# A fixed order for the first stage: query products, then key products, between the transposes of the input tiles

## The chip, the cores and the metric

The kernel runs on one core of a Trainium2 (trn2) chip. The metric is the device time of one execution in microseconds (us); the time of a kernel is the median of several runs. TensorE (PE) does the matrix products, VectorE (DVE) and ScalarE (ACT) the elementwise work and the copies out of PSUM, GpSimd (POOL) sums between SBUF tiles, and SyncE's queue (SP) issues all DMAs. "PEld" in the profile is TensorE's weight load.

## The reference, cut to what matters

One pre-norm transformer block on x of 1 x 1024 x 512, in float32: attention with 32 heads of 128, then a feed-forward net whose weights are signs.

```
x = x + attn(layernorm(x), wq, wkv, wo)
x = x + ffn(layernorm(x), k0, s0, k1, s1, k2, s2)

attn: q, k, v = h @ wq, h @ wkv ...          # 32 heads, 128 used columns each
      p = softmax(q k^T * 192**-0.5, causal)
      out = (p v) @ wo
ffn:  h = relu(s0 * (x @ sign(k0))) * 2 ; h = relu(s1 * (ei(h) @ sign(k1))) * 2 ; s2 * (ei(h) @ sign(k2))
```

The change touches the first layer norm, the queries and keys of the first two heads, and three small constants of the feed-forward net.

## The kernel before, in words

The 1024 tokens are 8 tiles of 128. The heads are taken in pairs. The queries, keys and values of a pair are made in seven partial products of half size each (Strassen's scheme, `products`, L313); a generator spreads these products over the softmax steps of the pair before. The first pair has no pair before it, so its queries and keys are made plainly by `qk_plain` (L284), ahead of everything else; its values come from `products(2, 0)` during the first pair's softmax steps.

**The first stage.** SP issues the loads in program order (L106 to L109): x tile 0, wq of head 0, x tile 1, wq of head 1, x tile 2, wk of head 0, x tile 3, wk of head 1, x tiles 4 to 7; then the value weights `wv` (L148), `wo` (L150), a second copy of x into `acc` (L158) and the three scalars `s_sb` (L164). A DMA may have to wait for the one eight places before it. For each tile of x, `statistics` (L201) makes mean and variance on DVE (bn_stats, bn_aggr), the root on ACT (L215) and its reciprocal on DVE (L217); `normalise` (L220) applies them on DVE; `transposed` (L226) makes four PE transposes into one PSUM bank of the pool `ps_mm`; and ACT copies that bank into `xnT` (L236). `qk_plain(0)` and `qk_plain(1)` then make, for each half of the tokens, four banks: queries of heads 0 and 1, keys of heads 0 and 1. A unit, as it is called below, is one tile of tokens in one bank: four products of 128 x 128, which the trace shows as eight matmul rows (a float32 product runs as two). Three banks are from pool `ps_st` (3 buffers), the fourth from `ps_sc`, the pool of one buffer that the softmax scores use. ACT copies each full bank to `qT` or `kT` (L306).

Then POOL makes `token_sums` (L248), four sums over `xnT` that the partial products read; the last of them overwrites a half of `xnT` in place, so it waits for the plain products. The first softmax step (`softmax_step`, L611) follows: scores on PE, minimum on DVE (L485), exponential on ACT (L496), scale (L501), and block transposes on DVE into `tb` (L507). SP exchanges blocks of `tb` into `pT` by 16 or 32 DMAs (L551), which the value product `ps_av` reads.

**What sets the order.** Each engine runs its own queue in order. A scheduler in the tile framework orders instructions that are not pinned; `pinned[0]` turns on program order for matmuls (`matmul`, L64 to L68). Before the change it is turned on after the first softmax step (L629), so the whole first stage is ordered by the scheduler. On PE it put the transposes of the tiles first, with a few products between them. PSUM has `ps_sc` 1, `ps_st` 3 and `ps_mm` 3 buffers.

Of the kernel before, what the change touches and what calls it, by code (L numbers as in the profile page):

```python
# [29 lines left out]
def kernel(  # L30
# [30 lines left out]

    pinned = [False]

    def matmul(*args, **kw):  # L64

        ins = nc.tensor.matmul(*args, **kw)  # L66
        if pinned[0]:
            tc.keep_in_program_order(ins)  # L68

    def pool(name, bufs, **kw):  # L70
        return ctx.enter_context(tc.tile_pool(name=name, bufs=bufs, **kw))
# [15 lines left out]
    def load_x(t):  # L87
        if t % TPB == 0:
            x_in.append(pairs.tile([P, TPB, D], F32, tag="pT", name=f"x_in{t // TPB}", bufs=3))
        nc.sync.dma_start(x_in[-1][:, t % TPB, :], x_v[:, t, :])  # L90

    def load_qk_weights(which, g, heads_of=range(G)):
        if (which, g) not in w_raw:
            w_raw[which, g] = pairs.tile(
                [P, G, NC, DN], F32, tag="wraw", name=f"w{'qk'[which]}{g}"
            )
        for i in heads_of:
            h = g * G + i
# [7 lines left out]
    for t in range(NT):  # L106
# [27 lines left out]
        nc.gpsimd.memset(t, 0.0)  # L134
        tb.append(t)


    def load_v_weights(g):
        wv_sb[g] = pairs.tile([P, NC, G * DV], F32, tag="wv", name=f"wv{g}", bufs=1)
        first = H * DN + g * G * DV  # L140
        nc.sync.dma_start(wv_sb[g], wkv_v[:, :, first : first + G * DV])
# [6 lines left out]
    load_v_weights(0)  # L148
    load_qk_weights(0, 1)
    load_o_weights(0)  # L150


    acc = const.tile([P, 7, TPB, DH], F32, tag="acc", name="acc")
    xs = []
    for t in range(NT):
        k, i = divmod(t, TPB)
        xs.append(acc[:, 2 * k : 2 * k + 2, i, :])
        nc.sync.dma_start(xs[t], x_v[:, t, :].rearrange("p (h d) -> p h d", h=2))  # L158

    nc.gpsimd.tensor_tensor(acc[:, 2], acc[:, 2], acc[:, 3], ALU.subtract)  # L160

    s_sb = const.tile([P, 3], F32, tag="s", name="s_sb")
    for i, s in enumerate((s0, s1, s2)):
        nc.sync.dma_start(s_sb[:, i : i + 1], s[None, :].to_broadcast((P, 1)))  # L164
    s_twice = const.tile([P, 2], F32, tag="s_twice", name="s_twice")
    nc.vector.tensor_scalar_mul(s_twice, s_sb[:, 0:2], 2.0)


    mixed = n_exc // P
    f = const.tile([P, 1], F32, tag="f", name="f")  # L170
    nc.gpsimd.memset(f, 1.0)
    nc.gpsimd.affine_select(
        out=f,
        in_=f,
        compare_op=ALU.is_gt,
        fill=inh,
        base=n_exc - mixed * P,
        pattern=[[0, 1]],
        channel_multiplier=-1,
    )  # L180
    f_twice = const.tile([P, 1], F32, tag="f_twice", name="f_twice")
    nc.vector.tensor_scalar_mul(f_twice, f, 2.0)
    f_minus = const.tile([P, 1], F32, tag="f_minus", name="f_minus")
    nc.vector.tensor_scalar_mul(f_minus, f, -1.0)

    def sign_weights(i, k, slots):

# [13 lines left out]
    def statistics(tiles, name):  # L201

        n = len(tiles)
        mv = small.tile([P, n, 2], F32, tag=f"mv{n}", name=f"mv_{name}")
        for t, xt in enumerate(tiles):
            if len(xt.shape) == 2:
                stats = small.tile([P, 6], F32, tag="stats", name=f"stats_{name}{t}")
                nc.vector.bn_stats(stats, xt)
# [4 lines left out]
            nc.vector.bn_aggr(mv[:, t, :], stats)  # L213
        std = small.tile([P, n, 1], F32, tag=f"std{n}", name=f"std_{name}")
        nc.scalar.activation(std, mv[:, :, 1:2], AF.Sqrt, bias=eps)  # L215
        rstd = small.tile([P, n, 1], F32, tag=f"rstd{n}", name=f"rstd_{name}")
        nc.vector.reciprocal(rstd, std)  # L217
        return [(mv[:, t, 0:1], rstd[:, t, :]) for t in range(n)]

    def normalise(xt, mean_rstd, name):  # L220
        xn = work.tile([P, D], F32, tag="p", name=f"xn_{name}")
        dst = xn if len(xt.shape) == 2 else xn.rearrange("p (h d) -> p h d", h=2)
        nc.vector.tensor_scalar(dst, xt, *mean_rstd, ALU.subtract, ALU.mult)
        return xn

    def transposed(t, xn, name):  # L226
        pt = ps_mm.tile([P, NC, P], F32, tag="mm", name=f"ptx_{name}{t}")
        for c in range(NC):
            nc.tensor.transpose(pt[:, c, :], xn[:, c * P : (c + 1) * P], ident)
        return pt  # L230

    xnT = const.tile([P, NC, S], F32, tag="xnT", name="xnT")
    for t in range(NT):
        xt = x_in[t // TPB][:, t % TPB, :]
        xn = normalise(xt, statistics([xt], f"a{t}")[0], f"a{t}")
        nc.scalar.copy(xnT[:, :, t * P : (t + 1) * P], transposed(t, xn, "a"))  # L236

# [39 lines left out]
    def new_qk(which, h):  # L277
        dst = (qT, kT)[which]
        dst[h] = heads.tile(
            [P, S], F32, tag=("qT", "kT")[which], name=f"{'qk'[which]}T{h}", bufs=(4, 3)[which]  # L280
        )
        return dst[h]

    def qk_plain(k):  # L284


        outs = [(which, h) for which in range(2) for h in range(G)]
        if k == 0:
            for which, h in outs:
                new_qk(which, h)  # L290
        banks = [ps_st.tile([P, QB], F32, tag="st", name=f"ps_qk{k}_{n}") for n in range(3)]
        banks.append(ps_sc.tile([P, S], F32, tag="sc", name=f"ps_qk{k}_3")[:, :QB])
        for t in range(TPB):
            tok = slice(t * P, (t + 1) * P)
            for (which, h), ps in zip(outs, banks):
                for c in range(NC):
                    matmul(
                        ps[:, tok],
                        lhsT=w_raw[which, 0][:, h, c, :],
                        rhs=xnT[:, c, k * QB + t * P : k * QB + (t + 1) * P],  # L300
                        start=(c == 0),
                        stop=(c == NC - 1),
                        skip_group_check=True,
                    )
        for (which, h), ps in zip(outs, banks):
            nc.scalar.activation(  # L306
                (qT, kT)[which][h][:, k * QB : (k + 1) * QB],
                ps,
                AF.Copy,
                scale=(-scale, 1.0)[which],  # L310
            )

    def products(which, g):  # L313

# [275 lines left out]
        if qb == 1 and g + 2 < NG:  # L590
            attn_sums(g, early=(j == 0))

    for half in range(NQB):
        qk_plain(half)
    token_sums()
    weight_sums(2, 0)

    def products_of_pair(g):
        yield from products(2, g)
        if g + 1 < NG:  # L600
# [24 lines left out]
    PRODUCT, O_PART = 2.0, 1.0  # L625
    ATTEND_AFTER = (TPB, TPB + 2)

    softmax_step(*steps[0])
    pinned[0] = True  # L629
    for i, (h, qt) in enumerate(steps):  # L630
        g, j = divmod(h, G)
        s = i % (G * NT)
# [228 lines left out]
```

## Time and profile before

| what | value |
|---|---|
| median of 3 runs | 1369.76 us (1369.54 to 1373.94) |
| profiled execution, its own time | 1375.12 us |
| span of the profiled execution | 1373.3 us |
| PE busy | 1349.3 us, 98% of the span |
| DVE, ACT, POOL busy | 803.3, 495.9, 267.9 us |
| the chain that ended last, by engine | PE 94%, SP's queue 3%, DVE 1%, DMA 1% |
| PE's first instruction | at 8.09 us |
| first row of the second product stage (X_v) | at 48.67 us |

Between the span and the execution's own time lie 1.8 us. The first stage fills the first 48 us of 1373, so the profile page's 40 slices show it as little more than one slice. It has to be read from the timeline, which lists the instructions of all engines in order of start: start, duration, engine, line, operation, names (out<-in), shape, count, and in square brackets how long the engine had been idle and what ended that. Merged rows of matmuls count their pipelined ends, so the pace of a run of matmuls is (duration less one matmul's duration) over (count less one). A second view gives the busy time of each engine and TensorE's granted clock in chosen stretches.

### The profile page before, as it was taken

The page shows a single profiled execution, that of the slowest core. Times are in us where ns is not written, and L with a number is a line of the kernel's source. Part 1 is how long each engine was busy: PE and PEld are TensorE (multiplying, and loading weights), DVE is VectorE, ACT ScalarE, POOL GpSimd, SP SyncE. Part 2 cuts the span into 40 slices and gives each one's busy share as a digit, 9 for nine tenths or more (in the row PEclk, how much of TensorE's full clock was granted, in tenths as well). Part 3 has the DMA queues.
Part 4 walks back from the last instruction along what each step waited for, and adds up shares of the span by engine and source line. Part 5 has one row for each costly group of instructions (what it writes and reads, how often), then busy time and mean ns, then how long its engine had stood idle before and what let it go on. Part 6 is the DMA issues. An engine that isn't in the chain of part 4 may idle for free.

```text
span 1373.3 us, 16933 instructions
## 1 busy us (share of the span) xinstructions
PE 1349.3 (98%) x5564; PEld 872.3 (64%) x5564; DVE 803.3 (58%) x1658; ACT 495.9 (36%) x921; POOL 267.9 (20%) x326
## 2 busy tenths in 40 slices
PE   7998999999999999999999999999999999998998
PEld 6846566575756657575665757575665757655467
DVE  3364565656556565655656565665656656675475
ACT  2343333333434333333333333333333333344322
POOL 6201221221222212022221202222120212110200
PEclk9999999999999999999999999999999999999999
DMA  5234444443444444343444434344443434334201
GB/s 184 57 89 108 102 105 109 99 119 96 111 104 113 101 108 107 97 119 96 114 103 112 108 96 116 96 110 106 111 108 95 119 93 113 98 93 110 73 1 62
DMA packets 267446, 139.33 MB, mean 101 GB/s; under 512 B 26208, under 2 KB 261216, under 8 KB 267360
## 3 DMA queue, kind: packets, MB, share of 16 engines
q1 hardware_dynamic: 267360, 138.25, 39.7%
q8 instruction: 45, 0.74, 0.3%
q14 instruction: 41, 0.34, 0.1%
HBM read 38.54 MB, written 2.10 MB: 30 GB/s over the span
## 4 chain that ended last, share of the span: by engine, by line
PE 94%; SPq 3%; DVE 1%; DMA 1%; ACT 0%; issue 0%; ACTq 0%
PE ps_av L66 18%; PE sc L66 17%; PE ps_o L66 14%; PE Y_v L66 6%; PE Y_q L66 5%; PE Y_k L66 5%; PE X_v L66 4%; PE Z_v L66 4%; PE X_q L66 4%; PE Z_q L66 4%; PE X_k L66 3%; PE Z_k L66 3%; SPq L551 3%; PE ps_qk L66 2%; PE ps_h L66 2%; PE ps_out L66 1%
## 5 line engine op out<-in xcount | busy, mean ns | idle before, releaser
L496 ACT ACTIVATE p<-p,nmax 128x128 f32<-128x128 f32 (+7 forms) x256 | 198.3, 775 | 679.1 <-DVE nmax L485 677.2
L66 PE MATMUL sc<-kT,qT 128*128 128x512 f32 (+3 forms) x768 | 290.8, 488 | 3.4 <-DVE nmax L485 2.7
L66 PE MATMUL ps_av<-pT,v 128*128 128x512 f32 x744 | 254.4, 492 | 4.6 <-DMA pT<-tb 4.6
L485 DVE CUSTOM_DVE_ANT_0 p<-sc,mask 128x128 f32<-128x128 f32 (+7 forms) x256 | 191.5, 748 | 103.4 <-PE sc L66 103.2
L507 DVE STREAM_TRANSPOSE tb<-p 128x128 f32<-128x128 f32 (+1 forms) x248 | 187.1, 769 | 83.9 <-ACT p L501 77.3
L501 ACT ACTIVATE p<-p,rtotal 128x128 f32<-128x128 f32 (+7 forms) x256 | 196.4, 772 | 92.8 <-DVE rtotal L500 92.8
L66 PEld LDWEIGHTS ps_av<-pT,v 128*128 128x128 f32 x744 | 142.7, 192 | 134.5 <-issue 105.8
L66 PEld LDWEIGHTS sc<-kT,qT 128*128 128x128 f32 x768 | 138.8, 191 | 91.9 <-issue 77.0
L448 DVE TENSOR_TENSOR acc<-acc,ps_o 128x512 f32<-128x512 f32 x190 | 128.9, 683 | 56.1 <-PE ps_o L66 50.9
L66 PE MATMUL ps_o<-wo,attn 128*128 128x256 f32 (+1 forms) x400 | 111.1, 414 | 0.0
L500 DVE RECIPROCAL rtotal<-total 128x1 f32<-128x1 f32 x256 | 40.5, 158 | 109.6 <-ACT p L496 109.3
L66 PEld LDWEIGHTS ps_o<-wo,attn 128*128 128x128 f32 x400 | 73.3, 190 | 30.6 <-issue 23.4
L409 POOL TENSOR_TENSOR at<-attn,attn 128x512 f32<-128x512 f32 x14 | 17.7, 1266 | 348.4 <-DVE attn L589 348.4
L264 POOL TENSOR_TENSOR wsumk<-wk 128x256 f32<-128x256 f32 x15 | 10.9, 727 | 306.8 <-DMA wk<-in_L_attn_wkv_dram 271.6
L589 DVE COPY attn<-ps_av 128x512 f32<-128x512 f32 x62 | 42.3, 682 | 41.2 <-PE ps_av L66 41.2
L66 PEld LDWEIGHTS X_v<-wv,xnT 128*128 128x128 f32 x512 | 62.4, 192 | 5.2
L66 PE MATMUL X_v<-wv,xnT 128*128 128x128 f32 x512 | 62.4, 275 | 0.0
L66 PEld LDWEIGHTS ps_o<-osum,at 128*128 128x128 f32 x224 | 42.5, 190 | 22.8 <-issue 19.1
L66 PE MATMUL X_q<-xnT,wq 128*128 128x512 f32 x120 | 56.4, 593 | 0.0
L66 PE MATMUL X_k<-xnT,wk 128*128 128x512 f32 x120 | 56.4, 592 | 0.0
L66 PE MATMUL ps_o<-osum,at 128*128 128x256 f32 x224 | 55.0, 379 | 0.0
L496 ACT ACTIVATION_READ_ACCUMULATOR p<-p,nmax 128x1 f32 x256 | 47.8, 187 | 0.0
(143 smaller groups left out, 1639.4 us busy)
## 6 DMA issues: line engine op xcount, KB each, us to landing
pT<-tb SPq DMA_DIRECT2D x1488, 64.0 KB, 2.0
wq<-in_L_attn_wq_dram SPq DMA_DIRECT2D x32, 256.0 KB, 3.3
wk<-in_L_attn_wkv_dram SPq DMA_DIRECT2D x32, 256.0 KB, 3.9
wv<-in_L_attn_wkv_dram SPq DMA_DIRECT2D x16, 512.0 KB, 4.0
wo<-in_L_attn_wo_dram SPq DMA_DIRECT2D x16, 512.0 KB, 3.9
x_in<-_attn_hidden_states_dram SPq DMA_DIRECT2D x8, 256.0 KB, 5.8
acc<-_attn_hidden_states_dram SPq DMA_DIRECT2D x8, 256.0 KB, 7.2
out_dram<-osb SPq DMA_DIRECT2D x8, 256.0 KB, 2.0
```

The lines of the kernel that those rows point to most:

```text
L66: ins = nc.tensor.matmul(*args, **kw)
L264: nc.gpsimd.tensor_tensor(t[:, 0], a(1, 0), a(1, 1), ALU.add)
L409: nc.gpsimd.tensor_tensor(t0, b(0, 1), b(0, 0), ALU.subtract)
L448: nc.vector.tensor_tensor(dst, dst, ps, ALU.add)
L485: nc.vector.tensor_tensor_reduce(out=p[:, :n], in0=sc[:, :n], in1=mask[:, S - n :], scale=1.0, scalar=BIG, op0=ALU.add, op1=ALU.min, accum ...
L496: nc.scalar.activation(p[:, :n], p[:, :n], AF.Exp, bias=nmax, scale=-1.0, accum_out=total)
L500: nc.vector.reciprocal(rtotal, total)
L501: nc.scalar.activation(p[:, :n], p[:, :n], AF.Copy, scale=rtotal)
L507: nc.vector.transpose(tb[qb][:, : qt + 1, :, i, :], p[:, :n].rearrange("p (c b k) -> p c b k", b=NB, k=B32))
L551: nc.sync.dma_start(pT[b * B32 : (b + 1) * B32, :, a, :, :], tb[qb][a * B32 : (a + 1) * B32, chunks, b, :, :],)
L589: nc.vector.tensor_copy(dst.rearrange("p (t a i) -> p a t i", a=NB, i=B32), ps)
```

## The change

The work is the same, but for one extra square root on a constant. Its order and its place differ:

- Loads: x tile 0, wq, x tile 1, wq, wk, wk, x tiles 2 to 4, wv, x tiles 5 to 7. `wo`, `acc` and the second pair's wq follow after the first stage in the program.
- An ACT square root on a constant `one` stands first, so that the table for it is loaded at the start.
- `qk_plain` is one function over all 32 units. It calls `normalised_input` for tile 0, 1, ... before the units 0, 2, 7, 10, 13, 16, 19, 22, and the first softmax step before unit 26. Queries of tiles 0 and 1 come before their keys; from tile 2 on, a tile's four units stand together.
- Everything in that stage is pinned to program order on every engine (`keep_order`), also statistics, roots, normalisation, transposes and the copies to `qT` and `kT`.
- The fourth bank comes from `ps_mm` and not from `ps_sc`.
- The constants of the feed-forward net (`s_sb`, `f` and what is made from them) are made at the first step of head 2.

In the order that the engines get, PE has: transposes of tile 0, units 0 and 1, transposes of tile 1, units 2 to 6, transposes of tile 2, and so on; the transposes of tile 4 stand behind unit 12 and those of tile 5 behind unit 15. ACT has: copy of tile 3, copy of bank 0 to `qT`, root of tile 4, copy of tile 4, copies of banks 1, 2 and 3, root of tile 5, copy of tile 5. DVE takes the tiles one after the other, each from statistics to normalisation. From the second softmax step on, the order of every engine is that of before, but for `f_twice`, `f_minus` and `s_twice` on DVE, `f` on POOL and the three `s_sb` loads on SP.

```diff
+    load_x(0)
+    load_qk_weights(0, 0, [0])
+    load_x(1)
+    load_qk_weights(0, 0, [1])
+    load_qk_weights(1, 0)
+    for t in range(2, NT):
         load_x(t)
-        if t < TPB:
-            load_qk_weights(t // G, 0, [t % G])
+        if t == TPB:
+            load_v_weights(0)
+    one = const.tile([P, 1], F32, tag="one", name="one")
+    nc.vector.memset(one, 1.0)
+    nc.scalar.activation(one, one, AF.Sqrt)
...
+    def ffn_constants():
+        for i, s in enumerate((s0, s1, s2)):
+            keep_order(nc.sync.dma_start(s_sb[:, i : i + 1], s[None, :].to_broadcast((P, 1))))
+        keep_order(nc.vector.tensor_scalar_mul(s_twice, s_sb[:, 0:2], 2.0))
+        keep_order(nc.gpsimd.memset(f, 1.0))
...
+    def normalised_input(t):
         xt = x_in[t // TPB][:, t % TPB, :]
         xn = normalise(xt, statistics([xt], f"a{t}")[0], f"a{t}")
-        nc.scalar.copy(xnT[:, :, t * P : (t + 1) * P], transposed(t, xn, "a"))
+        keep_order(nc.scalar.copy(xnT[:, :, t * P : (t + 1) * P], transposed(t, xn, "a")))
...
-    def qk_plain(k):
+    def qk_plain(tiles_at, last_at, last):
+        units = [(t, n) for ns in ((0, 1), (2, 3)) for t in (0, 1) for n in ns]
+        units += [(t, n) for t in range(2, NT) for n in range(2 * G)]
+        for t, n in units:
+            for new in tiles_at.get(n_units, ()):
+                normalised_input(new)
+            if n_units == last_at:
+                last()
+            n_units += 1
+            k, i = divmod(t, TPB)
+            which, h = outs[n]
+            if i == 0:
+                pl, tag = ((ps_st, "st"), (ps_mm, "mm"))[n == 3]
+                banks[n] = pl.tile([P, QB], F32, tag=tag, name=f"ps_qk{k}_{n}")
+            for c in range(NC):
+                matmul(
...
+            if i == TPB - 1:
+                keep_order(
+                    nc.scalar.activation(
...
-    softmax_step(*steps[0])
     pinned[0] = True
+    qk_plain(
+        {0: (0,), 2: (1,), 7: (2,), 10: (3,), 13: (4,), 16: (5,), 19: (6,), 22: (7,)},
+        26,
+        lambda: softmax_step(*steps[0]),
+    )
+    load_o_weights(0)
...
+        if h == 2 and qt == 0:
+            ffn_constants()
```

More of the change, by code (lines that the diff above doesn't have):

```diff
@@ L62, with keep_order, matmul @@
     pinned = [False]
-    def matmul(*args, **kw):
-        ins = nc.tensor.matmul(*args, **kw)
+    def keep_order(ins):
         if pinned[0]:
             tc.keep_in_program_order(ins)
+    def matmul(*args, **kw):
+        keep_order(nc.tensor.matmul(*args, **kw))
     def pool(name, bufs, **kw):
@@ L103, in load_qk_weights, with load_v_weights @@
             nc.sync.dma_start(w_raw[which, g][:, i, :, :], src)
-    for t in range(NT):
-        load_x(t)
-        if t < TPB:
-            load_qk_weights(t // G, 0, [t % G])
+    def load_v_weights(g):
+        wv_sb[g] = pairs.tile([P, NC, G * DV], F32, tag="wv", name=f"wv{g}", bufs=1)
+        first = H * DN + g * G * DV
+        nc.sync.dma_start(wv_sb[g], wkv_v[:, :, first : first + G * DV])
+    load_x(0)
[4 more added lines that the diff above has]
+    for t in range(2, NT):
+        load_x(t)
+        if t == TPB:
[3 more added lines that the diff above has]
+    nc.scalar.activation(one, one, AF.Sqrt)
     ident = const.tile([P, P], F32, tag="ident", name="ident")
@@ L135 @@
         tb.append(t)
[L138 to L141, printed above, removed]
     def load_o_weights(g):
@@ L146, in load_o_weights @@
         nc.sync.dma_start(wo_sb[g], wo_v[:, g * G : (g + 1) * G, :])
[L148 to L160, printed above, removed]
     s_sb = const.tile([P, 3], F32, tag="s", name="s_sb")
-    for i, s in enumerate((s0, s1, s2)):
-        nc.sync.dma_start(s_sb[:, i : i + 1], s[None, :].to_broadcast((P, 1)))
     s_twice = const.tile([P, 2], F32, tag="s_twice", name="s_twice")
-    nc.vector.tensor_scalar_mul(s_twice, s_sb[:, 0:2], 2.0)
     mixed = n_exc // P
[L170 to L179, printed above, removed]
-    )
[L181 to L184, printed above, removed]
+    f, f_twice, f_minus = (
+        const.tile([P, 1], F32, tag=n, name=n) for n in ("f", "f_twice", "f_minus")
+    )
+    def ffn_constants():
[3 more added lines that the diff above has]
+        keep_order(nc.gpsimd.memset(f, 1.0))
+        nc.gpsimd.affine_select(
+            out=f,
+            in_=f,
+            compare_op=ALU.is_gt,
+            fill=inh,
+            base=n_exc - mixed * P,
+            pattern=[[0, 1]],
+            channel_multiplier=-1,
+        )
+        nc.vector.tensor_scalar_mul(f_twice, f, 2.0)
+        nc.vector.tensor_scalar_mul(f_minus, f, -1.0)
     def sign_weights(i, k, slots):
@@ L207, in statistics @@
                 stats = small.tile([P, 6], F32, tag="stats", name=f"stats_{name}{t}")
-                nc.vector.bn_stats(stats, xt)
+                keep_order(nc.vector.bn_stats(stats, xt))
             else:
@@ L212, in statistics @@
                     nc.vector.bn_stats(stats[:, half, :], xt[:, half, :])
-            nc.vector.bn_aggr(mv[:, t, :], stats)
+            keep_order(nc.vector.bn_aggr(mv[:, t, :], stats))
         std = small.tile([P, n, 1], F32, tag=f"std{n}", name=f"std_{name}")
-        nc.scalar.activation(std, mv[:, :, 1:2], AF.Sqrt, bias=eps)
+        keep_order(nc.scalar.activation(std, mv[:, :, 1:2], AF.Sqrt, bias=eps))
         rstd = small.tile([P, n, 1], F32, tag=f"rstd{n}", name=f"rstd_{name}")
-        nc.vector.reciprocal(rstd, std)
+        keep_order(nc.vector.reciprocal(rstd, std))
         return [(mv[:, t, 0:1], rstd[:, t, :]) for t in range(n)]
@@ L222, in normalise @@
         dst = xn if len(xt.shape) == 2 else xn.rearrange("p (h d) -> p h d", h=2)
-        nc.vector.tensor_scalar(dst, xt, *mean_rstd, ALU.subtract, ALU.mult)
+        keep_order(nc.vector.tensor_scalar(dst, xt, *mean_rstd, ALU.subtract, ALU.mult))
         return xn
@@ L228, in transposed @@
         for c in range(NC):
-            nc.tensor.transpose(pt[:, c, :], xn[:, c * P : (c + 1) * P], ident)
+            keep_order(nc.tensor.transpose(pt[:, c, :], xn[:, c * P : (c + 1) * P], ident))
         return pt
     xnT = const.tile([P, NC, S], F32, tag="xnT", name="xnT")
-    for t in range(NT):
+    def normalised_input(t):
         xt = x_in[t // TPB][:, t % TPB, :]
         xn = normalise(xt, statistics([xt], f"a{t}")[0], f"a{t}")
-        nc.scalar.copy(xnT[:, :, t * P : (t + 1) * P], transposed(t, xn, "a"))
+        keep_order(nc.scalar.copy(xnT[:, :, t * P : (t + 1) * P], transposed(t, xn, "a")))
     def B(j, k):
@@ L282, in new_qk @@
         return dst[h]
-    def qk_plain(k):
+    def qk_plain(tiles_at, last_at, last):
         outs = [(which, h) for which in range(2) for h in range(G)]
[L288 to L303, printed above, removed]
-                    )
[L305 to L311, printed above, removed]
@@ new lines, in qk_plain @@
+        for which, h in outs:
+            new_qk(which, h)
+        banks, n_units = {}, 0
+        units = [(t, n) for ns in ((0, 1), (2, 3)) for t in (0, 1) for n in ns]
[13 more added lines that the diff above has]
+                matmul(
+                    banks[n][:, i * P : (i + 1) * P],
+                    lhsT=w_raw[which, 0][:, h, c, :],
+                    rhs=xnT[:, c, t * P : (t + 1) * P],
+                    start=(c == 0),
+                    stop=(c == NC - 1),
+                    skip_group_check=True,
+                )
+            if i == TPB - 1:
+                keep_order(
+                    nc.scalar.activation(
+                        (qT, kT)[which][h][:, k * QB : (k + 1) * QB],
+                        banks[n],
+                        AF.Copy,
+                        scale=(-scale, 1.0)[which],
+                    )
+                )
@@ L591, in attend @@
             attn_sums(g, early=(j == 0))
[L593 to L596, printed above, removed]
     def products_of_pair(g):
@@ L626 @@
     ATTEND_AFTER = (TPB, TPB + 2)
-    softmax_step(*steps[0])
     pinned[0] = True
+    qk_plain(
+        {0: (0,), 2: (1,), 7: (2,), 10: (3,), 13: (4,), 16: (5,), 19: (6,), 22: (7,)},
+        26,
+        lambda: softmax_step(*steps[0]),
+    )
+    load_o_weights(0)
+    acc = const.tile([P, 7, TPB, DH], F32, tag="acc", name="acc")
+    xs = []
+    for t in range(NT):
+        k, i = divmod(t, TPB)
+        xs.append(acc[:, 2 * k : 2 * k + 2, i, :])
+        nc.sync.dma_start(xs[t], x_v[:, t, :].rearrange("p (h d) -> p h d", h=2))
+    nc.gpsimd.tensor_tensor(acc[:, 2], acc[:, 2], acc[:, 3], ALU.subtract)
+    token_sums()
+    weight_sums(2, 0)
+    load_qk_weights(0, 1)
     for i, (h, qt) in enumerate(steps):
```

## The prediction

> **What bounds the kernel now.** The page says PE 98% busy, and the chain that ended last is 94% PE. So the time falls by what PE's idle or slow stretches lose, and by nothing else. I then read the timeline of the first 75 us, where the change lies. Columns: start us, duration us, engine, line, operation, names, shape, count, and in brackets the idle time before and what ended it.
>
> ```profile
> 3.52 0.69 DVE L208 BATCH_NORM_STATS2 stats_a<-x_in 128x6 f32<-128x512 f32 x1 [3.52 <-DMA x_in<-_attn_hidden_states_dram]
> ...
> 4.51 1.28 ACT L215 ACT_TABLE_LOAD   x1 [4.51 <-DVE mv_a L213]
> ...
> 6.40 0.69 DVE L208 BATCH_NORM_STATS2 stats_a<-x_in 128x6 f32<-128x512 f32 x1 [1.97 <-DMA x_in<-_attn_hidden_states_dram]
> ...
> 7.23 0.13 DVE L217 RECIPROCAL rstd_a<-std_a 128x1 f32<-128x1 f32 x1
> ...
> 7.39 0.55 DVE L223 TENSOR_SCALAR xn_a<-x_in,mv_a,rstd_a 128x512 f32<-128x512 f32 x1
> ...
> 8.09 2.13 PE L229 MATMUL ptx_a<-ident,xn_a 128*128 128x128 f32 x8 [8.09 <-DVE rstd_a L217]
> ...
> 14.27 1.09 PE L229 MATMUL ptx_a<-ident,xn_a 128*128 128x128 f32 x4 [0.25 <-ACT xnT L236]
> ...
> 15.15 2.34 PE L66 MATMUL ps_qk<-xnT,wq 128*128 128x128 f32 x10
> ...
> 19.60 1.95 PE L66 MATMUL ps_qk<-xnT,wk 128*128 128x128 f32 x16
> ```
>
> PE's first transposes wait until 8.09. Tile 0 landed at 3.52, but two things delay its normalisation: the table load of 1.28 before ACT's root, and, behind that, DVE's queue: the statistics of tile 1 stand ahead of the reciprocal of tile 0, and tile 1 lands at 6.40. The reciprocal runs at 7.23, the normalisation at 7.39.
>
> The pace matters too. Ten product rows in 2.34 us are (2.34 - 0.42)/9 = 0.213 us each; from 19.60, sixteen in 1.95 are (1.95 - 0.275)/15 = 0.112 (0.42 and 0.275 are the lengths of one such row in the two stretches). Until about 18.4 PE runs at half pace, whatever the clock column says of that time.
>
> The end of the stage:
>
> ```profile
> 44.61 1.95 PE L66 MATMUL ps_qk<-xnT,wk 128*128 128x128 f32 x16
> ...
> 46.60 0.60 ACT L306 ACTIVATE kT<-ps_qk 128x512 f32<-128x512 f32 x1 [0.29 <-PE ps_qk L66]
> ...
> 47.25 0.49 PE L66 MATMUL sc<-kT,qT 128*128 128x128 f32 x2 [0.69 <-ACT kT L306]
> ...
> 48.13 0.70 PE L66 MATMUL sc<-kT,qT 128*128 128x256 f32 x2 [0.39 <-DVE nmax L485]
> ...
> 48.67 1.95 PE L66 MATMUL X_v<-wv,xnT 128*128 128x128 f32 x16
> ```
>
> The last product row starts at 46.29, its copy to kT ends at 47.20, then come the first scores, and the second scores wait for DVE to read the first, since they share one bank: 48.13. X_v starts at 48.67.
>
> Last, I read the granted clock in stretches (length, PE busy, count, clock, DMA share, GB/s), to learn which idle stretches cost pace:
>
> ```profile
> core 0: us, PE busy (x), PEclk, DMA share, GB/s
> ...
> 107.16:110.58 3.42, 1.26 (x4) 1.00 0.45 108
> 110.58:113.99 3.41, 1.94 (x3) 0.50 0.63 176
> 113.99:117.40 3.41, 3.41 (x10) 0.50 0.38 92
> 117.40:120.80 3.40, 3.40 (x32) 1.00 0.42 100
> 1250.62:1254.03 3.41, 1.39 (x4) 1.00 0.41 98
> 1254.03:1257.44 3.41, 3.06 (x4) 0.50 0.40 97
> ...
> 1312.06:1315.47 3.41, 1.94 (x15) 1.00 0.00 0
> ```
>
> A stretch of 3.4 us with PE busy 1.26 or 1.39 (37% and 41%) is followed by half clock; one with 1.94 (57%) isn't. Full clock comes back after a stretch that is nearly full.
>
> **The start, part by part.** All product and transpose rows stay: 256 product rows and 32 transpose rows, at full pace 256 x 0.1117 + 32 x 0.1095 = 32.1 us, plus two score rows, 0.22. What changes is start, idle time and half-paced rows.
>
> First transpose: mean and variance reach ACT at 4.51. With the table loaded earlier the root ends at 4.80 (0.29); reciprocal at 4.82, normalisation 0.16 later, PE 0.70 after that (7.39 to 8.09): 5.68, so 2.41 earlier. The extra memset and root on `one` run while DVE and ACT wait for x, before 3.5. If ACT's first load were late instead, it would cost at most its 1.28.
>
> Transposes of tile 0: four at 0.213, to 6.53; the last result 0.21 later, copy 0.59, hand-over 0.08: 7.41. Two query units, 16 x 0.213, to 10.82. The wq tiles are second and fourth DMA as before and do not stop this (the second was issued at 2.19 and landed within 5.0). Tile 1: landed 6.40, root from 7.39, normalised by 8.56, so ready; transposes 10.82 to 11.67. Now PE waits for their copy: 0.88, to 12.55.
>
> The clock: PE is without a gap from 7.41 to 11.67, 4.26 us. In before the gapless stretch from 14.27 to about 18.4, 4.15 us, brought full pace. I take full pace from 12.55. Here the Trainium skill has a rule (TensorE: Matmul & The Clock Gate, Part 1: The HAM clock gate): about 3.4 us of sustained work releases the clock, but counted in free-running windows[...]. By the row, pace is full at 12.55. By the rule, a stretch of 4.26 may miss a whole window, and the next chance ends up to 3.41 later, at 15.96: that is 16 rows at half pace, 1.7 us lost. Other phases lie between. The same chance hangs over before, whose full pace came early in its possible span (17.7 to 21.1).
>
> From 12.55 on: 240 product rows 26.81, 24 transpose rows 2.63, two score rows 0.22, so 42.2 without idle time.
>
> **Where a new wait comes in.** ACT's queue is in order. The copy of bank 0 to qT stands ahead of the root of tile 4, and it needs the whole of unit 12. The transposes of tile 4 stand on PE right behind unit 12. So PE waits for: last row's result 0.275, hand-over 0.04, copy on ACT 0.51 until the next can start, root 0.29, reciprocal 0.02 + 0.16, normalisation to PE 0.70: 1.98, less one row's 0.11, so 1.87 us. The same happens at tile 5: the copies of banks 1 to 3 stand ahead of its root, the last of them needs unit 15, and the transposes follow unit 15 at once. Queued behind these on PE are all remaining units. Tiles 2, 3, 6 and 7 do not have it: no bank copy stands between, and three or more units (0.9 us each) cover their copies. Tile 2 has one unit of 0.89 to cover the copy's about 0.8. Two waits, 3.74 us.
>
> Sum: 42.2 + 3.74 = 45.95 us at the end of the last unit. The second scores can start there, since DVE read the first long before, and the table for the exponential (1.28) loads under the units. In before they start at 48.13: 2.2 us gained. In parts: 2.4 from the earlier start, 1.5 at the end (48.13 less 46.40 and 0.22 of score rows), 1.4 from half-paced rows (24 for 38, 0.10 each), less 3.3 of idle time (5.5 for 2.2): 2.0, and the rest is rounding.
>
> **What I cost at nothing.** x tiles 2 to 7 now follow the wk tiles, and wv goes ahead of tile 5. At 362 GB/s (8 to 20 us) a tile takes 0.72, so tile 2 lands near 9.3, tile 4 near 10.7, wv near 12.2 and tile 7 near 14.4. PE asks for tile 2 after about 16.5 and for tile 7 after 36. Cover: 7 us or more; without it a tile's lateness counts fully. POOL's sums: tile 7 is copied near 37.4, T[0] and T[1] take 2.35 each plus gaps, 42.3; Y_v needs them near 48.2, so 6 us of cover. The last sum, in place, starts when the units end, as before, and has the same five microseconds to its use. `wo` and `acc` land by about 22 and are used much later; wq of the second pair waits for the last query unit, as before. The fourth bank from `ps_mm` leaves two buffers for transposes that are copied within 1 us.
>
> The constants at head 2: three DMAs of about 0.4 us on SP behind the second exchange of head 1 (about 135 in before), so wk, 16 exchanges and wv behind them come 1.2 to 1.3 later. The value product that reads those exchanges starts at 154.80, the exchanges were issued by 146.6: cover 5 us or more. SP then idles before the next group. On DVE `f_twice` stands ahead of the copy of `attn` at 116.69 and waits for POOL's `f` behind sums that end at 117.41: DVE is held to about 117.8, 1.1 us. The scores at 120.92 need the minimum that would now end near 119.1: cover 1.8. If PE comes there at full clock, up to 3 us earlier, about 0.8 would show. I take 0.
>
> **Rivals.** (1) The two waits drop the clock. Each leaves a 3.4 us stretch with PE busy 1.70 of 3.41, 50%, between 41% (dropped) and 57% (kept). The skill speaks against a drop (same page, HAM oscillation: it warns only of gaps over about 3.4 us, which makes this rival nothing), but the stretch to 1254.03 was followed by half clock with one gap of 2.37, so the row decides, and it leaves a chance. Price: after the drop at 110.58 PE worked 5.35 us at half clock, 2.7 lost. Twice is 5.4 less a little where only one stretch holds enough of a wait: 5.1. Time 2.9 above before, 1372.7. It decides from below about 50% busy.
>
> (2) More is gained. Either the waits at tiles 4 and 5 turn out hidden (then -5.9, 1363.9), or the later clock drops, at 110.58 and 1254.03, fall differently as PE's stalls move against the windows: at 110 between 3.4 and 6.8 us of half pace, so up to 1 gained, at 1254 up to 1.7, together -4.9, 1364.9. Against the first stands the order of the queues, which is certain. For the second speaks that runs of before differ by 4.4 us.
>
> (3) The change does not do what it says: the first stage is DMA-bound until tile 1 lands and only PE-bound after, and the gain of the start is eaten by late full pace (-0.4): 1369.3. It shades into the likeliest case.
>
> **The numbers.** In the profiled execution the sum gives 1375.12 - 2.2 = 1372.9. That execution is 5.4 above the median; the first stage is the same program, so the difference is taken from the median: 1369.76 - 2.2 = 1367.6. Chances: the likeliest case with (3), -0.4 to -3.5, 0.60; rival (1) 0.15; rival (2) 0.20; something slow that I do not see 0.05. The measurement tells about 0.3%, 4.1 us, from no change: below 1365.65 is faster, above 1373.9 slower. Faster comes from most of (2), 0.18; slower from the worst of (1) and the unseen, 0.10; the rest is within. Range from 1364.0, near the far end of (2), to 1372.6, near the sum of (1).
>
> **What would show it.** Right: PE's first row near 5.7; X_v near 46.4 in place of 48.67; two PE idle stretches of about 1.7 to 1.9 before the transposes of tiles 4 and 5, ended by DVE's normalisation, with the bank copy ahead of the root on ACT; full pace from about 12 to 16; no idle time between the last unit and the second scores. Wrong: half clock after those waits; a wait for an x tile or for T; PE held at 120 by DVE.

## The result and the profile after

| | before | after |
|---|---|---|
| median, measured side by side | 1371.84 us (1368.84 to 1374.51) | 1374.32 us (1372.04 to 1375.44) |
| after / before | | 1.0018, 95% interval 1.0010 to 1.0025 |
| profiled execution, its span | 1375.12, 1373.3 us | 1372.76, 1370.9 us |
| first transposes | 8.09 us | 8.06 us |
| first row of X_v | 48.67 us | 48.95 us |
| X_v of pair 1 to X_v of pair 2 | 68.63 us | 67.18 us |
| X_v of pair 2 to X_v of pair 3 | 79.68 us | 79.95 us |

The change is slower by about 2.5 us, where 2.2 us of gain were forecast. The two profiled executions alone would say the opposite (1372.76 against 1375.12): one execution carries more or fewer stretches of half clock than another, and the profiled one of before had three of them. So below, times come from many runs, and traces are compared stretch by stretch.

The start, from the timeline of the changed kernel (start us, duration us, engine, line, operation, names):

```profile
2.38 5.25 POOL L150 MEMSET tb<- 128x2048 f32 x2
...
4.76 0.16 DVE L215 RECIPROCAL rstd_a<-std_a 128x1 f32<-128x1 f32 x1 [0.43 <-ACT std_a L213]
4.96 2.95 DVE L221 TENSOR_SCALAR xn_a<-x_in,mv_a,rstd_a 128x512 f32<-128x512 f32 x1
...
8.06 1.09 PE L227 MATMUL ptx_a<-ident,xn_a 128*128 128x128 f32 x4 [8.06 <-DVE xn_a L221]
```

The early table load did its part: the reciprocal comes at 4.76 where 4.82 was forecast, against 7.23 before. But the normalisation behind it takes 2.95 us instead of 0.55. It ends at 7.91, just after POOL has finished clearing the two buffers `tb` (2.38 + 5.25 = 7.63). So the transposes start where they started before.

The middle, PE's rows alone:

```profile
27.54 0.63 PE L227 MATMUL ptx_a<-ident,xn_a 128*128 128x128 f32 x4 [1.81 <-DVE xn_a L221]
...
32.66 0.63 PE L227 MATMUL ptx_a<-ident,xn_a 128*128 128x128 f32 x4 [1.81 <-DVE xn_a L221]
```

These are the two waits that were forecast at tiles 4 and 5, at 1.81 us of idle time. And the end of the stage, with the second pair's beginning:

```profile
48.52 0.60 PE L70 MATMUL sc<-kT,qT 128*128 128x256 f32 x2
...
48.95 0.72 PE L70 MATMUL X_v<-wv,xnT 128*128 128x128 f32 x5
...
117.50 0.15 DVE L181 TENSOR_SCALAR f_twice<-f 128x1 f32<-128x1 f32 x1 [3.82 <-POOL f L172]
```

The second scores follow the last unit without a pause, as forecast, but at 48.52 instead of 45.95. At head 2 DVE is held for 3.82 us until POOL delivers `f`.

The granted clock of PE in stretches (length, PE busy, count, clock, DMA share, GB/s), cut where the clock changes:

```profile
core 0: us, PE busy (x), PEclk, DMA share, GB/s
...
109.03:112.45 3.42, 1.13 (x4) 1.00 0.55 140
112.45:115.87 3.42, 3.42 (x8) 0.50 0.44 118
```

After a stretch with PE busy 1.13 of 3.42 there is one at half clock, and near 1250 there is none; before had two near 110 and one near 1250. That, and not the first stage, makes this one execution the shorter one.

### The profile page after: what moved, and what is told of

It is laid out like the page before. It is cut to its first block, busy times and chain, and to the rows that moved or that the text cites. A ratio compares the mean times of both kernels' runs of the same rounds, so it can differ in the third digit from the quotient of the medians.

```text
span 1370.9 us, 16940 instructions
## 1 busy us (share of the span) xinstructions
PE 1344.8 (98%) x5564; PEld 869.5 (63%) x5564; DVE 805.7 (59%) x1659; ACT 496.1 (36%) x922; POOL 268.8 (20%) x326
## 4 chain that ended last, share of the span: by engine, by line
PE 96%; DVE 1%; SPq 1%; DMA 1%; ACT 1%; issue 0%; POOL 0%; DVEq 0%; POOLq 0%; ACTq 0%
PE ps_av L70 18%; PE sc L70 18%; PE ps_o L70 14%; PE Y_v L70 6%; PE Y_k L70 6%; PE Y_q L70 6%; PE X_v L70 4%; PE Z_v L70 4%; PE X_q L70 4%; PE Z_q L70 4%; PE X_k L70 4%; PE Z_k L70 4%; PE ps_qk L70 2%; PE ps_h L70 2%; PE ps_out L70 1%; SPq L562 1%
## 5 line engine op out<-in xcount | busy, mean ns | idle before, releaser
L263 POOL TENSOR_TENSOR wsumk<-wk 128x256 f32<-128x256 f32 x15 | 11.4, 757 | 305.6 <-DMA wk<-in_L_attn_wkv_dram 293.8
```

The lines of the kernel that those rows point to most:

```text
L263: nc.gpsimd.tensor_tensor(t[:, 0], a(1, 0), a(1, 1), ALU.add)
```

## The experiments

Theory P: the clearing of `tb` on POOL shuts DVE's normalisation out while it runs, so the start gains nothing. Theory K: the constants at head 2, costed at nothing, hold DVE and then PE. The two waits were forecast, so they only had to be sized. Rivals: the first transposes are held by something else (rival A: landing DMAs); the constants are harmless (rival N), and the moment at which the clock changes makes the difference. The other letters are explained in the expectation ahead of each run. All ratios are to the kernel before, with 95% intervals.

**e1, the clearing later.** It is tied behind the normalisation of tile 1.

```diff
-        nc.gpsimd.memset(t, 0.0)
...
+        if t == 1:
+            for z in tb:
+                nc.gpsimd.tensor_copy(z[:, 0, 0, 0, 0:1], xn[:, 0:1])
+                nc.gpsimd.memset(z, 0.0)
```

> The changed kernel, but POOL clears the two tb tiles only after the normalisation of tile 1 (a small POOL copy that reads it comes first). Theory P: DVE's normalisation of tile 0 took 2.95 us in place of 0.55 because POOL was clearing tb from 2.38 to 7.63 and the two cannot use the memory side by side; so it takes 0.55 here, the first transposes start at 5.6 to 5.7 and X_v 2.4 us earlier than 48.95 (46.5, up to 1.7 more or less where full pace comes at another moment), and the time falls by 2.4 from 1374.3 to about 1371.9, ratio to the kernel before 1.000. Rival A: it was slow because x and weight tiles were landing just then, whatever POOL did; then it stays near 2.9 us, first transposes at 8.06, time 1374.3, ratio 1.0018.

Measured: 1373.28 us, 1.0017 (1.0008 to 1.0027). The normalisation of tile 0 took 0.55 and the first transposes started at 5.83, but X_v only at 48.19. Its timeline shows why:

```profile
15.09 5.26 POOL L237 MEMSET tb<- 128x2048 f32 x2
...
18.88 1.75 DVE L220 TENSOR_SCALAR xn_a<-x_in,mv_a,rstd_a 128x512 f32<-128x512 f32 x1
...
24.02 2.34 POOL L653 TENSOR_TENSOR acc<-acc 128x1024 f32<-128x1024 f32 x1
25.23 1.41 DVE L220 TENSOR_SCALAR xn_a<-x_in,mv_a,rstd_a 128x512 f32<-128x512 f32 x1
```

The clearing now meets the normalisation of tile 3, and the subtraction `acc`, pushed back on POOL, meets that of tile 4; each ends just after POOL's instruction does (20.63 after 20.35, 26.64 after 26.36). PE's wait ahead of tile 4 grew from 1.81 to 2.70. P holds for the start. Its worth in time is not shown by this run, since the lock was moved and not removed: 1371.9 had been expected.

**e4, the clearing done twice.** The line is repeated in a loop of two.

> The changed kernel with each tb tile cleared twice on POOL, 5.25 us more of it. Theory P: the normalisation of tile 0 ends near 13.2, the first transposes start at 13.3, everything behind is 5.2 us later: about 1379.5, ratio 1.0056 (or 1 to 2 us less where full pace comes in a better moment). Rival A: normalisation of tile 0 still ends at 7.9, ratio 1.0018.

Measured: 1380.58 us, 1.0061 (1.0041 to 1.0080).

```profile
2.37 10.45 POOL L151 MEMSET tb<- 128x2048 f32 x4
...
5.17 7.93 DVE L222 TENSOR_SCALAR xn_a<-x_in,mv_a,rstd_a 128x512 f32<-128x512 f32 x1
```

The normalisation again ends (13.10) just after the clearing (12.82), PE's first transposes move to 13.25, and the whole program follows by about 6 us (four executions). Landing DMAs as the cause are out: the loads are the same, and in e7 below, where the DMA engines were as busy from 2 to 8 us (share 1.00, in after 1.02), the normalisation took 0.55.

**e7, the clearing on DVE.** It is cut into three pieces of 1.76 us that stand in DVE's idle time.

```diff
-        nc.gpsimd.memset(t, 0.0)
...
+        for z in {2: (tb[0],), 3: (tb[1][:, :4],), 4: (tb[1][:, 4:],)}.get(t, ()):
+            keep_order(nc.vector.memset(z, 0.0))
```

> The clearing of both buffers tb leaves POOL for good: DVE does it in its own idle time, in three pieces behind the normalisations of tiles 2, 3 and 4. Theory P (in the change the clearing on POOL holds back the first normalisation): the normalisation of tile 0 takes 0.55 us at about 5.1 us, the first transposes start at 5.8 instead of 8.06, no later normalisation is held back by a clearing (only the addition acc on POOL may lengthen one, to at most 1.4 us), the two waits of 1.81 us before the transposes of tiles 4 and 5 stay, X_v starts at 46.7 instead of 48.95, and the time falls by the whole 2.2 us: 1372.1, about 1.0000 to 1.0005 of before. Rival G (the start's gain is given back inside the stage whatever is done with the clearing, because the moment of the full clock and not the first transposes sets the stage): X_v at 48 or later, 1373.3 as with the clearing moved behind tile 1, 1.0015 of before.

Measured: 1372.22 us, 1.0001 (0.9989 to 1.0014).

```profile
5.19 0.55 DVE L220 TENSOR_SCALAR xn_a<-x_in,mv_a,rstd_a 128x512 f32<-128x512 f32 x1
```

PE starts at 5.88, 0.14 after the normalisation ends (in after 0.15), and X_v at 47.19, 1.8 us sooner than after. This is P's number (1372.1), not the rival's (1373.3, or 1.0015, just above the interval): with the lock gone and not merely moved, the start's gain reaches the end.

**e2, the roots early.** Statistics, root and normalisation of tiles 4 and 5 are issued before units 12 and 13, so that they stand ahead of the bank copies in ACT's queue.

```diff
+            if n_units in (12, 13):
+                prepare(n_units - 8)
             for new in tiles_at.get(n_units, ()):
```

> The changed kernel, but statistics, root and normalisation of tiles 4 and 5 are put before units 12 and 13, ahead of the copies of the full banks on ACT. If the two PE waits of 1.81 us are in full on the path: both vanish, X_v at 45.3, time 3.6 us lower, 1370.7, ratio 0.9992. Rival: they are partly given back by the clock (the waits make no difference to the clock, but what stands behind them may meet another stretch): a change between 1.5 and 5 us.

Measured: 1370.38 us, 0.9995 (0.9987 to 1.0002). Both waits are gone. X_v stands at 47.42, not at the expected 45.3, because full clock came only at 19.43 in this trace (13.47 in after). The ratio is 0.0019 to 0.0023 below that of the changed kernel (its two comparisons gave 1.0014 and 1.0018), 2.6 to 3.2 us. The two waits had been costed at 3.74.

**e3, the constants early.** `ffn_constants()` is called before `token_sums()`, unpinned.

> The changed kernel, but the constants of the feed-forward net are made in the first stage again, in scheduler order, with their three loads behind those of acc. Theory C: at head 2 f_twice held DVE for 3.8 us (113.7 to 117.5), and that costs PE 0.2 us in the profiled execution and more where the clock does not drop at 112; time 0.3 to 1.0 lower than 1374.3: 1373.3 to 1374.0, ratio 1.0011 to 1.0016. Rival: DVE's slack takes it all, ratio 1.0018.

Measured: 1372.27 us, 1.0009 (0.9999 to 1.0020), about 1.2 us below after. The interval still holds the rival's 1.0018, so this run alone does not decide. In its trace the second pair's interval is 79.62 again.

**b2, the constants late and nothing else.** In the kernel before, the loads of `s_sb`, `s_twice`, `f`, `f_twice` and `f_minus` move into the first step of head 2, pinned as in the change; the order of everything else stays.

```diff
+        if h == 2 and qt == 0:
+            ffn_constants()
```

> The kernel before with one part of the change alone: the loads of s_sb, s_twice, f, f_twice and f_minus issued at head 2. The order of all else is that of before. Theory F: f stands on POOL behind the sums of the second pair's query weights, which wait for the weights' transfer, and comes at about 115.3 us whatever PE does; DVE waits for it with the eviction and the maxima behind it. An execution with a drop near 110 us loses 0.3 us in the second pair (interval 79.9), one without loses about 2.1 (interval 81.7), because PE is 1.7 us further by then. So the executions near 1369.3 go (to about 1371.3) and the others stay: the median rises by 0.5 to 1.5 us, 1.0004 to 1.0011 of before. Rival N (the late constants cost nothing that counts): executions at 1369 to 1369.5 are as many as in before, ratio 1.0000.

**b1, the kernel before**, unedited, for a trace beside it.

> The kernel before, unedited, one look. Theory F (the executions of one kernel differ by the clock's drops near 110 and 1253 us alone): the first-pair interval from X_v to X_v is 65.2 us without a drop near 110, 67.2 with one window of 3.41 us, 68.7 with two; the second pair's interval is 79.6 us in every case, since f_twice is made in the first stage; the time is 1369.3 without any drop, 1371.7 with one, 1375 with three windows. X_v stands at 47 to 49 according to the moment of the full clock.

Measured: b2 1373.67 us, 1.0015 (1.0007 to 1.0023); b1 1369.57 us. Neither trace has half clock near 110 us, so the two can be laid over each other. Before, at that place:

```profile
113.14 0.69 DVE L589 COPY attn<-ps_av 128x512 f32<-128x512 f32 x1 [0.36 <-PE ps_av L66]
...
116.94 0.81 PE L66 MATMUL sc<-kT,qT 128*128 128x384 f32 x2
```

And with the constants late:

```profile
116.31 0.19 POOL L180 TENSOR_SCALAR_AFFINE_SELECT f<-f 128x1 f32<-128x1 f32 x1
116.53 0.15 DVE L189 TENSOR_SCALAR f_twice<-f 128x1 f32<-128x1 f32 x1 [3.46 <-POOL f L180]
...
116.66 0.68 DVE L595 COPY attn<-ps_av 128x512 f32<-128x512 f32 x1
...
117.74 0.91 PE L66 MATMUL sc<-kT,qT 128*128 128x384 f32 x2 [0.46 <-DVE nmax L491]
```

`f` stands on POOL behind the sums of the second pair's query weights, which begin when those weights have come. DVE waits for `f_twice`, the eviction of `attn` starts 3.35 us later against PE (116.66 for 113.14, less the 0.17 by which PE stood later), and with it the maxima that PE's scores need; those scores, at 116.94 before, start at 117.74, and more is lost behind them. The second pair's interval is 81.57 against 79.63: 1.9 us. The trace of e7, which has the constants late and no half clock near 110 either, shows the same in the changed kernel: 81.79, so 2.2. In after, with half clock near 112, PE arrives later by itself and only 0.3 shows (79.95). Rival N is out: the interval of b2 lies above 1.0000, and of 53 executions of before 20 had a mean granted clock of 1.000, of b2's 22 none.

**a2, the changed kernel again**, unedited.

> The changed kernel once more, nothing edited. Theory C (windows of 3.41 us that run free of the program decide when the clock is full): the order of all instructions is the same, yet the first full-clock record may stand at another place than 13.47 us (up to 17 to 21), X_v moves with it by up to 3 us (49 to 52), and the first-pair interval X_v to X_v is 65.2, 67.2 or 68.9 according to whether the drop near 110 us is absent, one window or two. If instead the stage is the same to 0.3 us in every execution (rival D), full clock stands at 13.5 again and X_v at 49.0. The time is 1374.3 either way, 1.0018 of before.

Measured: 1374.08 us, 1.0014 (1.0003 to 1.0024); full clock at 13.18, X_v at 48.80, half clock once near 112, second interval 80.02. These two traces agree to 0.3 us, as rival D has it. But e2 has the same PE work up to this place and still ran at half pace there. Its four transposes, and below them those of after:

```profile
13.39 1.06 PE L227 MATMUL ptx_a<-ident,xn_a 128*128 128x128 f32 x4
...
13.40 0.65 PE L227 MATMUL ptx_a<-ident,xn_a 128*128 128x128 f32 x4
```

So the moment of full clock does wander between executions of equal work, here by 6 us (13.47 and 19.43).

**e8, clearing on DVE, roots early, constants early.**

> The clearing on DVE as in the run beside it, the statistics, roots and normalisations of tiles 4 and 5 issued before units 12 and 13, and the constants of the feed-forward stage back at the head of the program. If the three losses add (theory S): against the change 2.2 less at the start, 3.6 less for the two waits, 0.4 less for f_twice in the second pair, so 1374.3 - 6.2 = 1368.1, 0.9975 of before; X_v at about 43.5, X_v of the second pair 79.6 after that of the first-but-one as in before. If they hide one another (rival H: behind the waits lies another bound, a weight's transfer or the token sums on POOL), it is no better than moving the roots alone: 1370.4, 0.9995 of before, with a wait for a DMA or for POOL named in front of X_v or its units.

Measured: 1369.59 us, 0.9984 (0.9972 to 0.9997), 1.5 us above the 1368.1 at which the three gains would add. X_v stands at 46.43 and PE waits 2.87 us at tile 4:

```profile
22.16 2.34 POOL L660 TENSOR_TENSOR acc<-acc 128x1024 f32<-128x1024 f32 x1 [3.06 <-DMA acc<-_attn_hidden_states_dram]
22.43 2.10 DVE L167 TENSOR_SCALAR s_twice<-s_sb 128x2 f32<-128x2 f32 x1 [0.36 <-DMA s_sb<-in_L_ffn_s_dram]
...
26.00 0.63 PE L226 MATMUL ptx_a<-ident,xn_a 128*128 128x128 f32 x4 [2.87 <-DVE xn_a L220]
```

The same lock again. A scaling of two columns takes 2.10 us because POOL subtracts meanwhile, and the whole chain of tile 4 stands behind it.

**e9, the same with the four units of each tile together.**

```diff
-        units = [(t, n) for ns in ((0, 1), (2, 3)) for t in (0, 1) for n in ns]
-        units += [(t, n) for t in range(2, NT) for n in range(2 * G)]
+        units = [(t, n) for t in range(NT) for n in range(2 * G)]
```

> As the three together, and the units of tiles 0 and 1 go tile by tile (queries and keys of tile 0, then of tile 1) instead of the queries of both tiles ahead of the keys. If PE's gaps behind the first two copies are what puts the full clock off (theory C), there is full clock by about 11 us and the stage ends about 1 us sooner than with the three alone: about 1367, 0.997 of before. Rival W (the key weights have not landed by the third unit): PE waits for the transfer of wk at about 8 to 10 us, the gap is longer than the one removed, and the time is 1 to 2 us above that of the three alone.

Measured: 1370.61 us, 1.0001 (0.9987 to 1.0014): not below e8. Rival W is out too: in the trace nothing waited for the key weights. Nor did the order bring full clock sooner: it came at 11.06, in e8 at 10.54. It is again `s_twice` (22.29, 1.94 us long), now with PE idle 3.30 us ahead of tile 4, and this time the clock went with it:

```profile
core 0: us, PE busy (x), PEclk, DMA share, GB/s
21.30:24.71 3.41, 1.10 (x10) 1.00 0.00 0
24.71:28.12 3.41, 2.42 (x12) 0.50 0.00 0
28.12:31.54 3.42, 3.42 (x18) 0.50 0.00 0
```

**e10, e8 with the costly meetings removed.** `f` and what is made from it at the head, `s_twice` at head 2 as in the change, `acc` behind the normalisation of tile 4, and the last piece of the clearing behind tile 7.

```diff
+        if t == 4:
+            keep_order(nc.gpsimd.tensor_copy(after_t4, xn[:, 0:1]))
...
-    nc.gpsimd.tensor_tensor(acc[:, 2], acc[:, 2], acc[:, 3], ALU.subtract)
+    keep_order(nc.gpsimd.tensor_tensor(acc[:, 2], acc[:, 2], acc[:, 3], ALU.subtract))
+    f_constants()
```

> The change with every lock and wait found so far taken away: tb is cleared by DVE behind the normalisations of tiles 2, 3 and 7; tiles 4 and 5 are prepared before units 12 and 13; f, f_twice and f_minus are made at the head, but s_twice and the loads of s_sb at head 2 as in the change; the subtraction acc on POOL follows the normalisation of tile 4 (a copy of one column on POOL ties it), so that no normalisation or scaling of DVE meets it. Theory S (the losses add, and the 3.14 us wait of the three together at 22.9 us was s_twice locked out by acc): no PE gap over 1.2 us between 13 and 44 us, X_v at about 43.5 to 44.5, second-pair interval 79.6, time 1369.6 - 2.5 = about 1367.1, 0.9966 of before. Rival H (another bound behind them): X_v at 46 or later, 1369.5, and a wait of over 1.2 us named in the first stage.

Measured: 1368.80 us (1365.50 to 1372.96), 0.9977 (0.9966 to 0.9989). X_v at 43.51, and no idle time of PE over 1.2 us between 13 and 44 us. One meeting is left: `acc` (24.20 to 26.56) met the normalisation of tile 5 (25.47, 1.37 long), but its transposes, at 27.25, did not wait for it. The stage is as expected; the median is 1.7 us above the expected 1367.1, and its trace has half clock near 108 and 1248 us.

**e11, the same with the units tile by tile.**

> The same with the four units of each tile together. Theory S with theory C: the drop of the clock at 24.7 us of the earlier gapless kernel followed a wait of 3.58 us that s_twice and acc made, and goes with it; PE has one gap less before 15 us; X_v at 42.5 to 44, time about 1366.5, 0.996 of before. Rival W (the key weights land too late for this order): PE waits for wk in front of the units of tile 0 or 1, and the time is at or above that of the kernel beside it.

Measured: 1366.17 us, 0.9964 (0.9953 to 0.9975).

```profile
23.47 0.63 PE L226 MATMUL ptx_a<-ident,xn_a 128*128 128x128 f32 x4
...
42.88 1.95 PE L70 MATMUL X_v<-wv,xnT 128*128 128x128 f32 x16
```

The transposes of tile 4 no longer wait and X_v stands 6.1 us sooner than after. This version beats both kernels: about 5 us under before. Whether the order of the units adds anything to e10 stays open, since the intervals overlap (full clock came at 12.72 in e10 and 12.85 here).

## Why the prediction was wrong

It said 2.2 us faster, 1367.6; measured were 2.5 slower, 1374.3. Of these 6.7 us, 2.1 are the base: three runs gave 1369.76 for before, twenty gave 1371.84. The rest, 4.6, is in the sum.

**The first transposes: the step that failed.** The sum put the normalisation 0.16 after the reciprocal and PE 0.70 after that, 5.68, and so 2.41 us gained. The reciprocal came when it said; the normalisation lasted 2.95, and PE started at 8.06. The 0.70 was copied from a row of before in which the normalisation happened to run at 7.39, when POOL's clearing was nearly over; moved to 4.96 it met the clearing. Before carried the same bound, and its timeline has the clearing's row, which the working did not read. In b1, the kernel before once more, the normalisation began earlier and PE did not:

```profile
2.37 5.25 POOL L134 MEMSET tb<- 128x2048 f32 x2
...
7.12 0.83 DVE L223 TENSOR_SCALAR xn_a<-x_in,mv_a,rstd_a 128x512 f32<-128x512 f32 x1
...
8.09 1.09 PE L229 MATMUL ptx_a<-ident,xn_a 128*128 128x128 f32 x4 [8.09 <-DVE rstd_a L217]
```

It took 0.83 in place of 0.55 and ended at 7.95, after the clearing's 7.62. What the page of the Trainium skill, SBUF — State Buffer, in its section "Who interferes with whom", says was not weighed: POOL shares a port pair with DVE, and whichever of a POOL operation and a DVE operation in a two-port mode (`tensor_scalar` is named) starts first holds the pair for its whole length. The runs agree: 2.95 with one clearing, 7.93 with two, 0.55 with none. e7 prices the step: 1.0001 against 1.0014 for the same kernel beside it and 1.0018 in the first comparison, so 1.8 to 2.3 us, where the interval of e7 alone is 1.7 us to either side; in the traces the first transposes come 2.2 and X_v 1.8 us sooner.

**The constants: costed at nothing.** The working had the chain right (DVE held at `f_twice` behind POOL's sums), named "about 0.8" for the case in which PE comes at full clock, and took 0. It is 0.3 us in a trace with half clock near 112, and 1.9 (b2) and 2.2 (e7) in traces without. The profile of before, from which the 0 was taken, had two stretches of half clock there. Measured as a whole: 1.0015 when done alone (b2), 0.0005 to 0.0009 of ratio when undone alone (e3), so 0.7 to 2.1 us, with wide intervals. The first step and this one together are 2.5 to 4.4 of the 4.6 us.

**The waits at tiles 4 and 5: right.** Forecast 1.87 each (the terms as written add to 2.00, not 1.98, which makes it 1.89), 1.81 of idle time measured, and 1.98 lost from start to start (2.09 less one row's 0.11). Rival (1), that they drop the clock, did not come. In after, the stretches with most of the wait at tile 4 and with all of that at tile 5:

```profile
core 0: us, PE busy (x), PEclk, DMA share, GB/s
23.71:27.12 3.41, 2.02 (x19) 1.00 0.00 0
30.54:33.95 3.41, 1.60 (x15) 1.00 0.00 0
```

PE was busy 59% and 47%, and full clock stayed. The second is the worst that one such wait can do alone, since 3.41 less the whole 1.81 is 1.60. The two waits lose more than the better ending gains (1.5 in the working).

**Full pace: 6.9 us after PE's first row forecast (12.55 less 5.68), 5.4 measured (13.47 less 8.06).** A small gain, and luck: e2, with the same work up to there, took 11.4.

**The end: right.** No pause between the last unit and the second scores. 45.95 became 48.52; 2.38 of the 2.57 is the start.

**Loads, POOL's sums, fourth bank: right.** No wait for an x tile, for T or for a bank appeared.

So the change itself has a better ending, two new waits, and constants in a worse place, and the gain that should have paid for them was locked behind a clearing that the diff does not touch and the forecast did not look at.

What stays open is the rest of 0.2 to 2.1 us and why executions without any half clock became rare. With the constants late, 2 executions of 126 had a mean granted clock of 1.000; with them (or `f` alone) early, 21 of 80 in the changed kernels, and 20 of 53 in before. A reason can be argued: DVE's stall moves the idle spot near 1250 us against the one near 110 by 1.8 us (last matmul row before the idle time: 106.75 and 1247.43 in b1, 107.04 and 1249.55 in b2), so that the 3.41 us windows which step over one then meet the other. It was not tried.

## What to carry to other kernels

Before you move an operation of DVE to an earlier time, list what POOL does at that time, small clearings too: the duration in the old trace holds only for the old neighbours. Before you move a small constant to a "quiet" place, ask behind which transfers its producer will queue, and work the stall out for the case in which the consumer comes early. And take the base from many runs: a sum may be right about a stage and still be set against an execution that carries another set of clock drops.

## What the runs showed of the hardware

*The lock.* DVE's `tensor_scalar` on 128 x 512, met by a POOL operation, ended 0.28 us after it, however much longer than 0.55 that made it: 2.95, 7.93 and 1.75 us against a clearing, 1.41 against a two-input subtraction. On 128 x 2 it ended 0.03 after the subtraction and took 2.10 (e8), for 0.13 at 139.57 in after with nothing beside it. Not everything was held: the statistics (0.69 at 3.43 us in after) ran at full speed beside the clearing, so did the reciprocal (0.16), and `f_twice`, a `tensor_scalar` on 128 x 1, took 0.14 at 16.57 in before, inside a POOL sum of 16.32 to 17.23. And it works the other way round: in after the normalisation at 21.01 stood first and took its 0.55, and the subtraction on POOL that began at 21.17 took 2.60, where it took 2.34 in e1.

*The clock.* Laid on each execution's own grid of 3.413 us (the recorded changes of the clock are all multiples of that apart), the 14 traces obey one rule. All 17 full-clock windows with PE busy 24% to 41% were followed by half clock, and none with 47% or more; between the two no window fell. Half clock ended after windows with 88% or more, and after none with 84% or less (before the first recorded change, half clock is read from the pace of the rows). The place of PE's first row within the grid was spread over the whole of it. So the same gap of about 2 us costs nothing more in one execution and half of 3.41, 1.7 us, in another, by where it falls: from the X_v of pair 1 to that of pair 2 the kernel before took 65.33 us in b1, without a window of half clock near 110, and 68.63 in its first profile, with two.
